# Stage 6 of a gated cross-attention network: PSUM dealt in single banks, and exponentials and maxima taken head by head

## The chip, the cores and the metric

The kernel runs on one core of one Trainium2 chip. The metric is the device time of one execution in microseconds, and smaller is better. The time of a kernel is the median of its runs; times are told in microseconds (us) throughout, durations of single instructions in us or ns.

## The reference

Four layers, each a cross-attention followed by a feed-forward, each added to x behind a tanh gate. The kernel works through them as stages 0 to 7; only stage 6, the attention of the last layer, is touched in what it computes. It is this function, on 4 batches of 512 tokens with 32 heads of 16 elements:

```python
def _L3_xattn_ref(x, ctx, pos_map, ctx_pos_map, Wq, Wkv, Wout, bout):   # x: layernormed (4, 512, 512), ctx: (4, 512, 256)
    q = (x @ Wq).reshape(b, n, 32, 16)
    k, v = jnp.split(ctx @ Wkv, 2, axis=-1)           # each (4, 512, 32 heads, 16)
    q = apply_axial_rope(q, pos_map)
    k = apply_axial_rope(k, ctx_pos_map)
    logits = jnp.einsum('bqhd,bkhd->bhqk', q, k) * 16 ** -0.5
    w = jax.nn.softmax(logits, axis=-1)
    attn = jnp.einsum('bhqk,bkhd->bqhd', w, v).reshape(b, n, 512)
    return attn @ Wout + bout
x = x + jnp.tanh(g_xattn[3]) * _L3_xattn_ref(...)
```

All of it is in float32.

## The kernel before, in words

A tile framework records the instructions in the order of the Python code, gives each a priority by that order, and then puts them into one fixed order for each engine; semaphores between the engines follow from the tiles that they share. So the order on an engine is fixed before the kernel starts, and an instruction that waits holds back all that stand behind it on that engine. `self.together` writes the matmuls of a group so that they start side by side (`tie` fixes their order among themselves), and `after` makes the first of the group wait for named instructions. `high_priority` moves an instruction ahead of others in its engine's order.

**Stage 6 (`s6`).** The keys with their rotation, transposed, and the values were made in earlier stages (`keys`, `keyT`) and lie in DRAM. Each head takes 32 rows of a 128-partition tile, so that four heads stand on four row groups of TensorE. Softmax needs the maximum over the keys, which the kernel gets from a first set of products, query by key (`ps`, in `maxima`): VectorE takes the negative maximum of each row (`tensor_reduce`, L1663), TensorE transposes it (`turn`, L1634), and VectorE adds it into a spare row of the query tile (L1639). The second set of products is key by query (`pl`, L1754 to L1763); with the spare row the maximum is subtracted in the product itself, and ScalarE takes the exponential (`prs`, L1769). `weigh` multiplies the exponentials by the values into `av`, `norm` transposes and divides, `project` and `projected` apply the output weights and add to x.

**The loop.** Over batch b (4), group g of four heads (8), block k of 128 keys (4) and pair i of heads (1, then 0): 256 *slots*. In each slot one group of four matmuls with 512 columns starts together: two `pl` products for this slot, and two `ps` products for a slot that lies LEAD = 12 slots ahead. They stand on the four different row groups. Then follow, on TensorE, what the slot has beside: after an i = 1 slot (called odd below) the four `av` products of the block before (`later`), after an i = 0 slot (even) what is in `behind` (`norm`, `project`, `projected`), a `turn`, or a piece of the next batch's queries from `todo`: `xT` (transposes of the layernormed x), `query` (a product of 4 matmuls, then six rotation instructions of VectorE, L1427 to L1429), `queryT` (eight transposes and two copies).

**PSUM.** Eight banks of 512 floats a partition. `ps4` holds one `pl` tile of two banks; `ps2` holds two tiles `sc` of two banks each, for the `ps` products and for the pieces `xT` and `queryT` (and for `query` of the first batch); `ps1` holds one bank `mm` (turns, norms, projections, later queries) and one bank `av`. One instruction of ScalarE reads both banks of a `pl` tile, one of VectorE both banks of a `ps` tile. A group's first matmul waits for the exponential of the slot before, as there is one `pl` tile, and, by `freed[-2:-1]`, for the maximum of two slots before.

```python
yield parts, freed[-2:-1], after              # L1668, freed: the reduces so far
self.together(parts + more, freed)            # L1765
nc.scalar.activation(prs[i], pl, AF.Exp)      # L1769, [128, 2, 512]
```

Of the kernel before, what the change touches and what calls it, by code (L numbers as in the profile page):

```python
# [9 lines left out]
F32 = mybir.dt.float32  # L10
# [5 lines left out]
AF = mybir.ActivationFunctionType  # L16
ALU = mybir.AluOpType
AX = mybir.AxisListType

P = 128  # L20
NB = 4
S = 512
# [26 lines left out]
class Net:  # L49
# [1390 lines left out]
                self.nc.gpsimd.memset(r[:, :, 16:17], fill)  # L1440
        return rooms

    def headsT(self, name, r, put):

        v = r.rearrange("p (g h) k -> p g (h k)", g=8)
        pt = self.sc(f"pt_{name}")
        for y in range(2):
            for i in range(4):
                self.nc.tensor.transpose(
                    pt[:, y, i * P : (i + 1) * P], v[:, 4 * y + i, :], self.ident  # L1450
                )
        put(pt)

    VW = 32 * 17 + 15

# [74 lines left out]
    def keyT(self, b, k, r):  # L1530
        kt = self.kp.tile([P, 8, P], F32, tag="kt", name=f"s6_kt_{b}_{k}", bufs=2)

        self.headsT(
            f"s6k_{b}_{k}", r,
            lambda pt: self.nc.scalar.mul(
                kt.rearrange("p (y g) n -> p y (g n)", y=2), pt, 16**-0.5
            ),
        )
        self.nc.sync.dma_start(self.k6[b][:, :, k * P : (k + 1) * P], kt)

    def s6(self):
        nc, a = self.nc, self.a
# [5 lines left out]
        ropes = self.padded("s6_q", 2, None)  # L1548
# [3 lines left out]
        ]  # L1552
        LEAD = 12
        made, stats = {}, {}

        top = [
            self.vp.tile([P, TB, 4, 32], F32, tag=f"top{i}", name=f"s6_top{i}", bufs=1)
# [5 lines left out]
        def pieces(b):  # L1563

            kT, qT = halves("kT", b), halves("qT", b)
            va = self.vp.tile([P, TB, VW], F32, tag="v", name=f"s6_v_{b}")
            made[b] = kT, qT, va
            for y in range(2):
                nc.sync.dma_start(kT[y], self.k6[b][:, 4 * y : 4 * y + 4, :])
            nc.sync.dma_start(va, self.v6[b].rearrange("(k p) n -> p k n", p=P))  # L1570
            xs = self.x[b * TB : (b + 1) * TB]
            room = {}
            cols = lambda k: slice(k * P, (k + 1) * P)

            def xT(y):
                if y == 0:
                    mv, rs = stats[b]
                    room["xl"] = []
                    for i, x in enumerate(xs):
                        xl = self.t(f"s6_xl_{b}_{i}")  # L1580
                        nc.vector.tensor_scalar(
                            xl, x, mv[:, i, 0:1], rs[:, i : i + 1], op0=ALU.subtract, op1=ALU.mult
                        )
                        room["xl"].append(xl)
                    room["xT"] = self.up.tile([P, DC, S], F32, tag="xT", name=f"s6_xT_{b}")
                pt = self.sc(f"s6_ptx_{b}_{y}")
                for i in range(2):
                    for t in range(TB):
                        nc.tensor.transpose(
                            pt[:, i, cols(t)], room["xl"][t][:, cols(2 * y + i)], self.ident  # L1590
                        )
                nc.scalar.copy(room["xT"][:, 2 * y : 2 * y + 2, :], pt)

            def query(t):
                if b:
                    pq = self.mm(f"s6_pq_{b}_{t}")
                else:

                    pq = self.sc(f"s6_pq_{b}_{t}")[:, 0, :]
                self.chain(pq, [(room["xT"][:, c, cols(t)], wq[:, c, :]) for c in range(DC)])  # L1600
                self.rope(f"q_{b}_{t}", pq, b * TB + t, ropes[t % 2])

            def results():

                self.combine("s5", self.wt5, range(b * TB, (b + 1) * TB))
                stats[b] = self.lnstats(
                    f"s6_{b}", self.x[b * TB : (b + 1) * TB], f"s6{b}", root=False
                )

            def queryT(t):  # L1610
                def put(pt):
                    for y in range(2):
                        nc.scalar.copy(
                            qT[y][:, :, cols(t)], pt[:, y, :].rearrange("p (g n) -> p g n", g=4)
                        )

                self.headsT(f"s6q_{b}_{t}", ropes[t % 2], put)

            out = [results, lambda: xT(0), lambda: xT(1)]
            for t in range(TB):  # L1620
                out.append(lambda t=t: query(t))
                if t:
                    out.append(lambda t=t: queryT(t - 1))
            return out + [lambda: None, lambda: queryT(TB - 1)]

        def maxima():

            freed = []

            def turn(b, g):  # L1630
                qT = made[b][1][g // 4]
                pt = self.mm(f"s6_ptm_{b}_{g}")
                for t in range(TB):
                    nc.tensor.transpose(  # L1634
                        pt[:, t * P : (t + 1) * P],
                        top[g % 2][:, t].rearrange("p j k -> p (j k)"),
                        self.ident,
                    )
                nc.vector.tensor_tensor(qT[:, g % 4, :], qT[:, g % 4, :], pt, op=ALU.add)  # L1639

            waiting = None
            for b in range(NB):
                kT, qT = made[b][0:2]
                for g in range(8):
                    for t in range(TB):
                        for y in range(2):
                            if waiting and t == 1:
                                turn(*waiting)
                                waiting = None
                            ps = self.sc(f"ps_s6_{b}_{g}_{t}_{y}")  # L1650
                            parts = []
                            for i in range(2):
                                rows = slice(32 * (2 * y + i), 32 * (2 * y + i + 1))
                                parts.append((
                                    ps[:, i, :],
                                    qT[g // 4][rows, g % 4, t * P : (t + 1) * P],
                                    kT[g // 4][rows, g % 4, :],
                                    dict(start=True, stop=True),
                                ))

                            def after(ps=ps, dst=top[g % 2][:, t, 2 * y : 2 * y + 2, 16:17]):
                                with self.tc.high_priority():
                                    i = nc.vector.tensor_reduce(  # L1663
                                        dst, ps, axis=AX.X, op=ALU.max, negate=True
                                    )
                                freed.append(i.ins)

                            yield parts, freed[-2:-1], after  # L1668
                    waiting = b, g
            turn(*waiting)  # L1670

        behind, later = Behind(), Behind()
        avs, o4s = {}, {}

        def flush(what):
            last, what.waiting = what.waiting, []
            for f, args in last:
                f(*args)

# [62 lines left out]
        for b in range(NB):  # L1742
# [4 lines left out]
            for g in range(8):  # L1747
                y, gi = g // 4, g % 4
                for k in range(TB):
                    prs = [None, None]  # L1750
                    for i in (1, 0):


                        pl = self.ps4.tile([P, 2, S], F32, tag="pl", name=f"pl_s6_{b}_{g}_{k}_{i}")  # L1754
                        parts = []
                        for j in (2 * i, 2 * i + 1):
                            rows = slice(32 * j, 32 * (j + 1))
                            parts.append((
                                pl[:, j % 2, :],
                                kT[y][rows, gi, k * P : (k + 1) * P],  # L1760
                                qT[y][rows, gi, :],
                                dict(start=True, stop=True),
                            ))  # L1763
                        more, freed, after = next(beside, None) or ([], [], None)
                        self.together(parts + more, freed)  # L1765
                        prs[i] = self.up.tile(
                            [P, 2, S], F32, tag="pr", name=f"pr_s6_{b}_{g}_{k}_{i}", bufs=4
                        )
                        nc.scalar.activation(prs[i], pl, AF.Exp)  # L1769
                        if after:  # L1770
                            after()
                        if i == 1:
                            flush(later)
                            later(weigh, b, g, k, prs, more=True)
                        else:
                            flush(behind)
                        slot += 1
                        while i == 0 and todo and (count - len(todo)) * room < slot * count:
                            todo.pop(0)()
# [72 lines left out]
def kernel(ctx: ExitStack, tc: tile.TileContext, a: dict, out: bass.AP):  # L1852
# [31 lines left out]
    net.y2 = 2  # L1884
    with net.pools(op=1, ep=4, bp=1, up=3, tp=8, sp=2, ps2=2, ps1=4):
        net.s5()
    with net.pools(wp=2, kq=4, vp=2, up=1, rp=1, tp=8, bp=1, sp=2, ps4=1, ps2=2, ps1=1):
        net.s6()
    net.y2 = 4
    with net.pools(op=1, wp=6, bp=1, up=6, tp=8, sp=2, ps2=2, ps1=4):  # L1890
# [84 lines left out]
```

## Time and profile before

| | |
|---|---|
| median of 3 runs | 3427.65 us (3422.73 to 3428.2) |
| the profiled execution, its own time | 3434.39 us |
| its span, first to last instruction | 3432.6 us |
| mean granted TensorE clock | 0.919 |
| TensorE busy (matmuls) | 2878.5 us, 84% |
| VectorE busy | 1960.6 us, 57% |
| ScalarE busy | 1180.2 us, 34% |
| stage 6: first of its transposes | 2282.20 us |
| stage 6: first and last exponential start | 2333.6 and 3016.2 us |

Times within the profile count from the first instruction. A row of the instruction groups has the line, the engine, the operation, what it writes and reads with the shape, how often, then its busy time, the mean duration of one, and the idle time of its engine just before them with what ended that idle time. A row of the timeline has the start, the duration from the first to the last of a merged run of instructions, the engine and the group. PE is TensorE (PEld its weight loads), DVE is VectorE, ACT is ScalarE, POOL is GpSimd, SP is SyncE. A float32 matmul shows as two records.

### The profile page before, as it was taken

How to read it: one execution, taken by the hardware profiler on the slowest of the kernel's cores; microseconds unless marked ns; L12 is line 12 of the kernel's file. 1: busy time of each engine (PE TensorE's matmuls, PEld its weight loads, DVE VectorE, ACT ScalarE, POOL GpSimd, SP SyncE). 2: the span in 40 equal slices, each digit the busy share in tenths (PEclk: the TensorE clock that was granted, in tenths of full speed). 3: DMA queues.
4: the chain of work that ended last, by engine and by line, in shares of the span. 5: the costliest groups of instructions: out<-in, count | busy, mean ns of one | idle time of the engine just before them, and what ended most of it. 6: DMA issues, size and time to landing. Idle time of an engine off the chain costs nothing.

```text
span 3432.6 us, 39483 instructions
## 1 busy us (share of the span) xinstructions
PE 2878.5 (84%) x14620; PEld 1422.3 (41%) x14624; DVE 1960.6 (57%) x2892; ACT 1180.2 (34%) x1663; POOL 626.3 (18%) x509
## 2 busy tenths in 40 slices
PE   4889898968899989998837699958888888889995
PEld 2333332223444444444415588832232322244673
DVE  5556555558898979975686211157555565434103
ACT  2243334355544444433222111113444344411231
POOL 0000000005564656650000122100000000000341
PEclk9799999978999999999967799988999999979997
DMA  3000000057676877851212799960000000022698
GB/s 124 7 1 7 1 1 9 1 181 222 196 233 177 229 204 232 243 168 56 75 60 93 236 325 320 316 216 11 13 27 13 26 1 1 1 74 77 232 384 318
DMA packets 266334, 438.52 MB, mean 128 GB/s; under 512 B 32368, under 2 KB 114544, under 8 KB 264608
## 3 DMA queue, kind: packets, MB, share of 16 engines
q1 hardware_dynamic: 247776, 382.52, 35.2%
q0 software_dynamic: 13760, 45.10, 3.6%
q10 hardware_dynamic: 4608, 8.39, 0.7%
q8 instruction: 116, 1.90, 0.2%
q14 instruction: 74, 0.61, 0.1%
HBM read 370.79 MB, written 65.13 MB: 127 GB/s over the span
## 4 chain that ended last, share of the span: by engine, by line
PE 35%; ACT 7%; DVE 6%; issue 3%; DMA 2%; POOL 2%; SPq 0%; POOLq 0%; ACTq 0%; DVEq 0%
PE s_po L238 8%; PE pl_s L262 8%; PE pg_s L238 6%; ACT pr_s L1769 6%; PE s_ph L238 2%; PE s_pq L238 2%; DVE x L729 1%; PE s_pr L238 1%; DMA s_y<-s_ys 1%; PE s_pkv L238 1%; PE pt_s L218 1%; POOL s_ys L1321 1%; PE s_av L262 1%; DVE st_s L175 1%; PE s_pb L238 1%
## 5 line engine op out<-in xcount | busy, mean ns | idle before, releaser
L262 PE MATMUL pl_s<-s_qT,s_kT 32*128 32x512 f32 (+1 forms) x1536 | 450.4, 663 | 128.3 <-ACT pr_s L1769 100.8
L1012 POOL TENSOR_TENSOR s_h<-s_h,s_C 128x512 f32<-128x512 f32 x256 | 445.7, 1741 | 300.8 <-DVE s_h L1011 261.6
L262 PE MATMUL ps_s<-s_kT,s_qT 32*128 32x512 f32 (+1 forms) x1536 | 453.9, 680 | 6.4 <-DVE s_nmx L599 4.1
L1663 DVE TENSOR_REDUCE s_top<-ps_s 128x2 f32<-128x1024 f32 x256 | 313.4, 1225 | 196.5 <-PE ps_s L262 196.3
L1769 ACT ACTIVATE pr_s<-pl_s 128x1024 f32<-128x1024 f32 x256 | 262.0, 1023 | 390.1 <-PE ps_s L262 359.4
L1011 DVE TENSOR_TENSOR_SCAN s_h<-s_da,s_db 128x512 f32<-128x512 f32 x256 | 311.9, 1218 | 62.8 <-PE s_y L262 36.9
L1010 ACT ACTIVATE s_da<-s_rdl,s_A 128x512 f32<-128x512 f32 x256 | 184.3, 722 | 333.0 <-DVE s_h L1011 331.0
L262 PEld LDWEIGHTS pl_s<-s_qT,s_kT 32*128 32x128 f32 (+1 forms) x1536 | 117.6, 187 | 408.9 <-ACT pr_s L1769 265.9
L238 PE MATMUL s_ph<-xT_s,s_wu 128*128 128x256 f32 x1024 | 248.4, 397 | 0.7 <-ACT xT_s L161 0.7
L771 PE MATMUL s_acc<-s_wd,s_hT 128*128 128x512 f32 x512 | 239.9, 612 | 6.7 <-ACT s_hT L802 6.7
L238 PEld LDWEIGHTS s_ph<-xT_s,s_wu 128*128 128x128 f32 x1024 | 198.4, 198 | 78.5 <-issue 48.3
L238 PEld LDWEIGHTS pg_s<-s_xbT,s_w 128*128 128x128 f32 (+1 forms) x1872 | 213.9, 183 | 19.8 <-issue 17.8
L599 DVE TENSOR_REDUCE s_nmx<-ps_s 128x2 f32<-128x992 f32 x128 | 151.3, 1184 | 119.3 <-PE ps_s L262 119.3
L238 PE MATMUL pg_s<-s_xbT,s_w 128*128 128x128 f32 (+1 forms) x1872 | 215.5, 275 | 1.4 <-ACT s_xbT L161 1.4
L262 PE MATMUL s_av<-pr_s,s_v 128*32 128x512 f32 (+1 forms) x1536 | 214.4, 632 | 1.2 <-ACT pr_s L1769 1.1
L1009 DVE TENSOR_TENSOR s_db<-s_B,s_rdu 128x512 f32<-128x512 f32 x256 | 204.3, 798 | 12.4 <-DMA s_B<-s_bc 4.6
L714 ACT ACTIVATE pr_s<-pl_s 128x1024 f32<-128x1024 f32 (+1 forms) x128 | 130.9, 1022 | 193.9 <-PE pl_s L262 163.5
L262 PE MATMUL s_y<-s_h,ident 64*64 64x512 f32 x1024 | 148.5, 643 | 51.4 <-issue 32.5
L1400 DVE TENSOR_TENSOR g_s<-g_s,pg_s 128x256 f32<-128x256 f32 x78 | 27.5, 352 | 263.8 <-ACT g_s L1399 263.8
L771 PEld LDWEIGHTS s_acc<-s_wd,s_hT 128*128 128x128 f32 x512 | 93.4, 192 | 151.9 <-issue 116.0
L1294 POOL DMA_INDIRECT s_xb<-s_xs,s_from x86 | 83.2, 967 | 371.6 <-PE ptr_s_xb L228 236.7
L1198 POOL IOTA s_js<- 128x39 f32 (+1 forms) x2 | 0.3, 174 | 778.9 <-PE s_po L238 778.9
(372 smaller groups left out, 4127.7 us busy)
## 6 DMA issues: line engine op xcount, KB each, us to landing
s_B<-s_bc SPq DMA_DIRECT2D x256, 256.0 KB, 4.9
s_C<-s_bc SPq DMA_DIRECT2D x256, 256.0 KB, 4.5
s_w<-in_s_wg SPq DMA_DIRECT2D x39, 704.0 KB, 4.8
s_w<-in_s_wu SPq DMA_DIRECT2D x39, 704.0 KB, 6.9
s_w_rt<-in_s_ru SPq DMA_DIRECT2D x47, 512.0 KB, 10.5
s_w_rt<-in_s_rd SPq DMA_DIRECT2D x47, 512.0 KB, 12.2
s_w<-in_s_wd SPq DMA_DIRECT2D x39, 512.0 KB, 8.4
s_y<-s_ys SPq DMA_DIRECT2D x32, 512.0 KB, 5.5
```

The costliest lines, as they stand in the source:

```text
L238: ins = self.nc.tensor.matmul(out, lhsT=l, rhs=r, start=(i == 0), stop=(i == len(pairs) - 1)).ins
L262: ins = self.nc.tensor.matmul(out, lhsT=l, rhs=r, **flags).ins
L599: i = nc.vector.tensor_reduce(nmx[:, at : at + 2], ps[:, :, 0:M], axis=AX.X, op=ALU.max, negate=True,)
L714: nc.scalar.activation(prs[i][0:n], pl[0:n], AF.Exp)
L771: ins = nc.tensor.matmul(accs[i][t], lhsT=hT[:, j, t * P : (t + 1) * P], rhs=wd[f // 4][:, f % 4, :], start=(f == 0), stop=(f == FC - 1),).ins
L1009: nc.vector.tensor_tensor(db, br, du, op=ALU.mult)
L1010: nc.scalar.activation(da, dl, AF.Exp, scale=am[:, e, n : n + 1])
L1011: nc.vector.tensor_tensor_scan(h, da, db, 0.0, op0=ALU.mult, op1=ALU.add)
L1012: nc.gpsimd.tensor_tensor(h, h, cr, op=ALU.mult)
L1294: self.nc.gpsimd.indirect_dma_start(out=t, out_offset=None, in_=self.sorted[name][1], in_offset=bass.IndirectOffsetOnAxis(ap=fr[:, j : j + ...
L1663: i = nc.vector.tensor_reduce(dst, ps, axis=AX.X, op=ALU.max, negate=True)
L1769: nc.scalar.activation(prs[i], pl, AF.Exp)
```

## The change

Stage 6's PSUM pools become one pool `ps3` with three buffers for each of two tags, every buffer a single bank: three banks `sc` for maxima and pieces, three banks `pl` for the weighed logits; `mm` and `av` stay. Every `pl` and `ps` product gets a bank of its own. The exponential and the maximum are taken by two instructions of 512 columns in place of one of 1024. A group's first matmul waits for `freed[-2:-1]` and `exps[-2:-1]`: as each slot now appends two entries, these are the first maximum and the first exponential of the slot just before. The pieces `xT` and `queryT` take two banks one after the other in place of one tile of two. `flush(behind, 2)` runs at most two of the waiting steps in a slot, and where nothing waited in `behind`, one more piece of `todo` is taken at once, so that the pieces come in earlier slots. `keyT` is written out in another way with the same instructions.

```diff
-    def headsT(self, name, r, put):
+    def headsT(self, name, r, y, pt):
         v = r.rearrange("p (g h) k -> p g (h k)", g=8)
-        pt = self.sc(f"pt_{name}")
-        for y in range(2):
-            for i in range(4):
-                self.nc.tensor.transpose(
-                    pt[:, y, i * P : (i + 1) * P], v[:, 4 * y + i, :], self.ident
-                )
-        put(pt)
+        for i in range(4):
+            self.nc.tensor.transpose(pt[:, i * P : (i + 1) * P], v[:, 4 * y + i, :], self.ident)
...
+        bank = lambda name: self.ps3.tile([P, S], F32, tag="sc", name=f"s6_{name}")
...
-                pt = self.sc(f"s6_ptx_{b}_{y}")
-                for i in range(2):
+                for c in (2 * y, 2 * y + 1):
+                    pt = bank(f"ptx_{b}_{c}")
                     for t in range(TB):
-                        nc.tensor.transpose(
-                            pt[:, i, cols(t)], room["xl"][t][:, cols(2 * y + i)], self.ident
-                        )
-                nc.scalar.copy(room["xT"][:, 2 * y : 2 * y + 2, :], pt)
+                        nc.tensor.transpose(pt[:, cols(t)], room["xl"][t][:, cols(c)], self.ident)
+                    nc.scalar.copy(room["xT"][:, c, :], pt)
...
             def queryT(t):
-                def put(pt):
-                    for y in range(2):
-                        nc.scalar.copy(
-                            qT[y][:, :, cols(t)], pt[:, y, :].rearrange("p (g n) -> p g n", g=4)
-                        )
-                self.headsT(f"s6q_{b}_{t}", ropes[t % 2], put)
+                for y in range(2):
+                    pt = bank(f"ptq_{b}_{t}_{y}")
+                    self.headsT(f"s6q_{b}_{t}", ropes[t % 2], y, pt)
+                    nc.scalar.copy(
+                        qT[y][:, :, cols(t)], pt.rearrange("p (g n) -> p g n", g=4)
+                    )
...
-                            ps = self.sc(f"ps_s6_{b}_{g}_{t}_{y}")
+                            ps = [bank(f"ps_{b}_{g}_{t}_{y}_{i}") for i in range(2)]
...
                             def after(ps=ps, dst=top[g % 2][:, t, 2 * y : 2 * y + 2, 16:17]):
-                                with self.tc.high_priority():
-                                    i = nc.vector.tensor_reduce(
-                                        dst, ps, axis=AX.X, op=ALU.max, negate=True
-                                    )
-                                freed.append(i.ins)
+                                for i in range(2):
+                                    with self.tc.high_priority():
+                                        ins = nc.vector.tensor_reduce(
+                                            dst[:, i], ps[i], axis=AX.X, op=ALU.max, negate=True
+                                        ).ins
+                                    freed.append(ins)
                             yield parts, freed[-2:-1], after
...
-        def flush(what):
-            last, what.waiting = what.waiting, []
+        def flush(what, n=None):
+            last, what.waiting = what.waiting[:n], what.waiting[n:] if n else []
...
-                        pl = self.ps4.tile([P, 2, S], F32, tag="pl", name=f"pl_s6_{b}_{g}_{k}_{i}")
+                        pl = [
+                            self.ps3.tile([P, S], F32, tag="pl", name=f"s6_pl_{b}_{g}_{k}_{i}_{j}")
+                            for j in range(2)
+                        ]
...
-                        self.together(parts + more, freed)
+                        self.together(parts + more, list(freed) + exps[-2:-1])
...
-                        nc.scalar.activation(prs[i], pl, AF.Exp)
+                        for j in range(2):
+                            exps.append(nc.scalar.activation(prs[i][:, j, :], pl[j], AF.Exp).ins)
...
-                            flush(behind)
+                            idle = not behind.waiting
+                            flush(behind, 2)
+                            if idle and todo:
+                                todo.pop(0)()
...
-    with net.pools(wp=2, kq=4, vp=2, up=1, rp=1, tp=8, bp=1, sp=2, ps4=1, ps2=2, ps1=1):
+    with net.pools(wp=2, kq=4, vp=2, up=1, rp=1, tp=8, bp=1, sp=2, ps3=3, ps1=1):
         net.s6()
```

More of the change, by code (lines that the diff above doesn't have):

```diff
@@ L1531, in keyT @@
         kt = self.kp.tile([P, 8, P], F32, tag="kt", name=f"s6_kt_{b}_{k}", bufs=2)
[L1533 to L1537, printed above, removed]
-        )
+        pt = self.sc(f"pt_s6k_{b}_{k}")
+        for y in range(2):
+            self.headsT(f"s6k_{b}_{k}", r, y, pt[:, y, :])
+        self.nc.scalar.mul(kt.rearrange("p (y g) n -> p y (g n)", y=2), pt, 16**-0.5)
         self.nc.sync.dma_start(self.k6[b][:, :, k * P : (k + 1) * P], kt)
@@ L1597, in query @@
                 else:
-                    pq = self.sc(f"s6_pq_{b}_{t}")[:, 0, :]
+                    pq = bank(f"pq_{b}_{t}")
                 self.chain(pq, [(room["xT"][:, c, cols(t)], wq[:, c, :]) for c in range(DC)])
@@ L1610, in queryT @@
             def queryT(t):
-                def put(pt):
-                    for y in range(2):
-                        nc.scalar.copy(
-                            qT[y][:, :, cols(t)], pt[:, y, :].rearrange("p (g n) -> p g n", g=4)
-                        )
-                self.headsT(f"s6q_{b}_{t}", ropes[t % 2], put)
+                for y in range(2):
+                    pt = bank(f"ptq_{b}_{t}_{y}")
[3 more added lines that the diff above has]
+                    )
             out = [results, lambda: xT(0), lambda: xT(1)]
@@ L1654, in maxima @@
                                 parts.append((
-                                    ps[:, i, :],
+                                    ps[i],
                                     qT[g // 4][rows, g % 4, t * P : (t + 1) * P],
@@ L1661, in after @@
                             def after(ps=ps, dst=top[g % 2][:, t, 2 * y : 2 * y + 2, 16:17]):
-                                with self.tc.high_priority():
-                                    i = nc.vector.tensor_reduce(
-                                        dst, ps, axis=AX.X, op=ALU.max, negate=True
-                                    )
-                                freed.append(i.ins)
+                                for i in range(2):
[4 more added lines that the diff above has]
+                                    freed.append(ins)
                             yield parts, freed[-2:-1], after
@@ L1672, in s6 @@
         behind, later = Behind(), Behind()
-        avs, o4s = {}, {}
-        def flush(what):
-            last, what.waiting = what.waiting, []
+        avs, o4s, exps = {}, {}, []
+        def flush(what, n=None):
+            last, what.waiting = what.waiting[:n], what.waiting[n:] if n else []
             for f, args in last:
@@ L1758, in s6 @@
                             parts.append((
-                                pl[:, j % 2, :],
+                                pl[j % 2],
                                 kT[y][rows, gi, k * P : (k + 1) * P],
```

## The prediction, made before the changed kernel ran

> **What bounds the kernel now.** I read the page's groups first, to see what stage 6 consists of and which engine waits for which; then the busy time by stretches, to see whether any engine is full; then the timeline of 12 us inside the loop, where the period can be read off. A row of the groups ends with the idle time before the instructions and who ended it.
>
> ```profile
> L262 PE MATMUL pl_s<-s_qT,s_kT 32*128 32x512 f32 (+1 forms) x1536 | 450.4, 663 | 128.3 <-ACT pr_s L1769 100.8
> L1663 DVE TENSOR_REDUCE s_top<-ps_s 128x2 f32<-128x1024 f32 x256 | 313.4, 1225 | 196.5 <-PE ps_s L262 196.3
> L1769 ACT ACTIVATE pr_s<-pl_s 128x1024 f32<-128x1024 f32 x256 | 262.0, 1023 | 390.1 <-PE ps_s L262 359.4
> ...
> L1613 ACT COPY s_qT<-pt_s6q 128x512 f32<-128x512 f32 x32 | 17.2, 588 | 19.5 <-PE pt_s6q L1449 19.5
> L163 DVE COPY xT_s<-pt_s 128x512 f32<-128x512 f32 x32 | 21.3, 685 | 32.5 <-PE pt_s L218 32.5
> ```
>
> TensorE waits for the exponential and the exponential waits for TensorE: a ring. The last two rows are the nearest to the new halves: 512 columns read from PSUM cost 0.588 us on ACT and 0.685 on DVE.
>
> ```profile
> 2400.00:2500.00 100.00, 81.91 (x572) 25.63 (x568) 59.86 (x68) 47.62 (x53) 0.00 (x0) 1.00 0.07 21
> 2800.00:2900.00 100.00, 85.64 (x560) 27.08 (x556) 57.95 (x61) 44.08 (x49) 0.00 (x0) 1.00 0.00 1
> ```
>
> Columns: width, then busy PE, PEld, DVE, ACT, POOL, then granted clock. No engine is full and the clock is 1.00.
>
> ```profile
> 2422.24 0.70 PE L262 MATMUL pl_s<-s_qT,s_kT 32*128 32x512 f32 x2 [0.17 <-ACT pr_s L1769]
> 2423.41 1.02 ACT L1769 ACTIVATE pr_s<-pl_s 128x1024 f32<-128x1024 f32 x1 [0.70 <-PE ps_s L262]
> 2423.47 1.23 DVE L1663 TENSOR_REDUCE s_top<-ps_s 128x2 f32<-128x1024 f32 x1 [1.09 <-PE ps_s L262]
> 2424.49 0.70 PE L262 MATMUL pl_s<-s_qT,s_kT 32*128 32x512 f32 x2 [0.52 <-ACT pr_s L1769]
> ...
> 2425.56 3.70 PE L238 MATMUL s_pq<-s_wq,s_xT 128*128 128x512 f32 x8
> ...
> 2429.19 1.06 PE L262 MATMUL s_av<-pr_s,s_v 128*32 128x512 f32 x8
> 2429.30 0.42 DVE L1427 TENSOR_TENSOR rt_q<-s_pq,s_sin 128x256 f32<-128x256 f32 x1 [2.35 <-PE s_pq L238]
> ...
> 2430.19 0.70 PE L262 MATMUL pl_s<-s_qT,s_kT 32*128 32x512 f32 x2
> ...
> 2431.09 0.42 DVE L1429 TENSOR_TENSOR s_q_r<-s_q_r,rt_q 128x256 f32<-128x256 f32 x1
> 2431.36 1.02 ACT L1769 ACTIVATE pr_s<-pl_s 128x1024 f32<-128x1024 f32 x1 [4.61 <-PE ps_s L262]
> 2431.43 1.22 DVE L1663 TENSOR_REDUCE s_top<-ps_s 128x2 f32<-128x1024 f32 x1
> 2432.44 0.70 PE L262 MATMUL pl_s<-s_qT,s_kT 32*128 32x512 f32 x2 [1.11 <-ACT pr_s L1769]
> 2433.51 1.07 PE L262 MATMUL s_av<-pr_s,s_v 128*32 128x512 f32 x8
> ...
> 2434.75 0.70 PE L262 MATMUL pl_s<-s_qT,s_kT 32*128 32x512 f32 x2 [0.17 <-ACT pr_s L1769]
> ```
>
> A group starts at 2422.24, its exponential 1.17 later (1.23 in other slots) and takes 1.02, the next group starts 0.06 after its end: 2.25; the slot from 2432.44 takes 2.31. Reading the whole loop this way, slots without large work alternate 2.31 (odd) and 2.25 (even). TensorE itself needs less: a group holds it 1.07 (2424.49 to 2425.56), a query 3.63 (to 2429.19), `av` 1.00 (to 2430.19). An odd slot on TensorE alone is 1.07 + 1.00 = 2.07. Slots with a query or a projection (4.70, or 5.70 with `av`) are TensorE's already.
>
> **The change part by part.**
>
> *The ring.* With three banks a slot needs one bank that is free and one that the first half-read of the slot before gives back. So the period becomes 1.23 + one half-read + 0.05. For ACT 0.588: 1.87. For DVE 0.69 (its tensor-tensor rows from PSUM cost 691 ns for 512 columns and 424 for 256, 1.04 ns a column, and 1.225 less 512 of these is 0.69; the copy is 0.685): 1.97, later than ACT. An odd slot is then TensorE's, 2.07; an even slot without large work is DVE's, 1.97. A pair goes from 4.56 to 4.04. The reduce of 512 columns isn't in the trace; its bounds are 0.57 (taking off at the rate between the 992- and 1024-column reduces, 1184 and 1225 ns, 1.28 ns a column) and 0.79 (the same 0.1 on the other side); I take 0.69, on which two rows agree. At 0.57 ACT's 1.87 is the limit.
>
> *The second halves.* In the trace two copies in a row take 1.07 together, so the pair of exponentials costs 1.07 against 1.02, and rotation instructions of DVE follow each other 0.08 before the last one's end, so the pair of maxima takes 1.30 against 1.225: 256 x 0.05 = 13 us on ACT and 256 x 0.075 = 19 on DVE. Nobody waits for the second half before the slot after next: it ends 2.53 after the group's start, the next maximum is due at 1.97 + 1.23 = 3.20. Cover: the next group's 1.23. Were it gone, each slot would pay 0.61.
> Here a rule speaks against the change. The Trainium skill, "TensorEngine Tiling (Array Packing)", section PSUM Bottleneck, advises to "Vectorize PSUM access across multiple tiles in same bank", and "Advanced Engine Details and Errata", section The Read-Write Bubble, advises large tiles because each instruction exposes the memory latency anew, and says that one instruction may read several banks: what the kernel before does. By the rule the split loses the larger of 13 and 19 us, which makes 3447, if these engines set the time. The rows say that ACT is 44 to 48% and DVE 58 to 60% busy here, and that what counts is the time to the first bank's release. I follow the rows.
>
> *What the lost slot of slack costs.* Before, a group waited for the maximum of two slots ago; now for that of the last. What stands on DVE ahead of a maximum now holds TensorE, and with it all that is queued behind the group: `av`, turns, transposes. In the order of the changed program the six rotations of a query stand ahead of the next slot's maxima. They start 0.11 after the query's end and let the next DVE instruction start 2.24 after it (2431.43 against 2429.19). The query now ends an even slot, so the next group starts at its end; its first maximum ends at 2.24 + 0.69 = 2.93, and the slot takes 2.98 in place of 2.07: 12 queries inside the loop. Norms (0.25 + 0.42) and turns (0.68) stand behind both maxima on DVE and end by 3.2, just when the next is due: nothing.
>
> *The pieces in single banks.* `queryT` takes two of three `sc` banks. The second must wait for the slot's first maximum (1.97), its transposes end at 2.40, and the next group's second `ps` product waits for the copy of the first, which stands on ACT behind both exponentials (1.23 + 0.49 + 0.49 = 2.21, plus 0.59, plus 0.05 = 2.85). I take 2.80 for such a slot, 3.05 with a turn behind it (0.64), against 2.25 and 2.53 before; bounds: 1.97 if the scheduler's order dodges the wait, 3.3 if it waits for the second copy. `xT` the same.
>
> *The new distribution.* In the order of the changed program all queries stand alone in even slots (4.70) where 9 of 12 stood with `av` (5.70). That only moves `av`; the sum below counts it.
>
> *Elsewhere.* keyT issues the same instructions. No DMA is added or moved past another; the loads of the next batch keep their place, and the DMA engines are nearly idle here (share 0.00 to 0.07).
>
> **The sum.** From the start at 2344.70 of one odd slot to that at 2978.60 lie 239 slots, 633.9 us. By the order of the changed program they are:
>
> - 98 odd with `av` alone at 2.07: 202.9
> - 12 odd after a query at 2.98: 35.8
> - 82 even (35 empty, 30 norms, 17 turns) and 3 with transposes of the output at 1.97: 167.4
> - 12 queries at 4.70: 56.4
> - 8 `queryT` at 2.80, 4 with a turn at 3.05, one `xT` at 3.1: 37.7
> - 7 projections at 4.70, 3 with `av` at 5.70, 5 slots of transposes and `av` (four at 2.65, one at 3.37, as before): 64.0
> - 4 mixed slots at batch changes, before 5.76 and 6.21, estimated 6.2 and 6.5: 25.4
>
> Together 589.6, a gain of 44.3. At the start of the loop, up to 2345, DVE sets the pace (residuals and maxima in a row), and the split costs 16 slots x 0.075 = 1, an earlier `xT` 0.5. At the end, ten slots without `ps` took 3.2 and 3.87 at a lower clock; five even ones save 1.02 - 0.59 = 0.43: 2. Gain 45. Against the profiled execution's 3434.4 that is 3389; it is 6.7 above the median of the runs, 3427.65, from which 3383 follows.
>
> **The rivals.**
>
> *DVE becomes the pacemaker (slower).* Its other work in a batch is about 38 us (rotations 4 x 2.2, turns 8 x 0.68, norms 8 x 0.67, projections 4 x 1.44, layernorm 4 x 0.54, the rest spread): 0.59 a slot. A maximum may be 2.28 - 1.97 = 0.31 late on average before the gain of a slot is gone. If all that work came ahead of maxima, a slot would take 1.97 + 0.59 = 2.56, 0.28 more than now in some 210 slots: +59, 3486. For it: DVE goes from 58 to some 82% of the shorter time, and the slack is one slot less. Against: the order puts nearly all but the rotations and a few projections behind the maxima.
>
> *Half the gain.* The piece slots wait for the second copy (13 x 0.5), and the even slots take 2.15 (83 x 0.18), because semaphores and two waits of a group add up: gain 23, 3405. For it: the 1.23 was never measured with two readers in a row on each engine.
>
> *More.* The half maximum takes 0.57, even slots 1.87 (85 x 0.1), the pieces dodge their wait (12 x 0.6): gain 60, 3368.
>
> *It does not do what it says:* the banks rotate so that a group needs the bank of the second read. Then a slot is 1.23 + 1.30 + 0.05 = 2.58, slower by about 60 as well. Against: each slot takes two of three banks and the pieces take two, so the first bank taken is always the one that is free.
>
> The granted clock could fall in a denser stage, but the stretch before stage 6 has TensorE 100% busy at 1.00, so no time is set on it.
>
> **How the numbers follow.** Forecast (gain 35 to 55) 0.58, half the gain 0.18, more 0.13, pacemaker 0.05, wrong rotation 0.03, no measurable change 0.03. A measurement of this kernel can tell about 0.2%, 7 us, from no change. Faster 0.88, same 0.04 (with the lowest end of half the gain, 0.01), slower 0.08. The range goes from the larger gain, with 4 us beyond it, to a gain of 17: 3364 to 3411.
>
> **What would show it.** In the changed profile: pairs of slots at 4.04; ACT rows of 128x512 at 0.59 and maxima at 0.69; the group's idle time ended by DVE's maximum in even slots and none in odd ones; slots after queries near 3.0; `queryT` slots near 2.8; stage 6 ending near 2975. Wrong if maxima start well after 1.23, if even slots stay at 2.2, or if the clock in 2400 to 2900 leaves 1.00.

## Result and the profile after

| | before | after |
|---|---|---|
| time, median of 4 runs each | 3426.32 us | 3398.16 us (3392.73 to 3401.39) |
| ratio | | 0.9917, 95% interval 0.99 to 0.9935 |
| span of the profiled execution | 3432.6 us | 3399.4 us |
| mean granted clock | 0.919 | 0.92 |

Faster by 28 us by the medians and by 33.2 us by the two profiled spans, where 44 to 45 were forecast. The time lies inside the range, and the mechanism is the one forecast, but the sum is made up differently.

The groups of the kernel after, from the page: busy time, mean ns of one instruction, then the idle time before it and who ended it.

```profile
L1656 DVE TENSOR_REDUCE s_top<-s_ps 128x1 f32<-128x512 f32 x512 | 330.1, 686 | 162.6 <-PE s_ps L262 158.4
L1766 ACT ACTIVATE pr_s<-s_pl 128x512 f32<-128x512 f32 x512 | 277.9, 595 | 344.2 <-PE s_ps L262 327.1
L262 PE MATMUL s_pl<-s_qT,s_kT 32*128 32x512 f32 x1024 | 291.4, 642 | 63.4 <-DVE s_top L1656 59.0
```

The halves cost what was assumed (686 ns for 0.69 us, 595 for 0.588). In the last row ACT no longer ends the group's waits: 59.0 of 63.4 us of them are now ended by the maximum. Before, in a row that holds products of other stages too, the exponential of stage 6 ended 100.8 of 128.3 us. The ring through the exponential is cut.

The busy time of the same two stretches as before (width, PE, PEld, DVE, ACT, POOL, granted clock, DMA share, GB/s):

```profile
2400.00:2500.00 100.00, 86.70 (x627) 27.15 (x620) 67.08 (x113) 54.81 (x101) 0.00 (x0) 1.00 0.03 11
2800.00:2900.00 100.00, 89.74 (x592) 28.64 (x588) 64.78 (x106) 49.81 (x93) 0.00 (x0) 1.00 0.00 1
```

TensorE rises from 82 to 87 and from 86 to 90. DVE stays below 70%, so it did not become the pacemaker.

The timeline of two slots of the loop after, an empty even one and an odd one with `av`:

```profile
2440.97 0.70 PE L262 MATMUL s_pl<-s_qT,s_kT 32*128 32x512 f32 x2
...
2442.12 1.08 ACT L1766 ACTIVATE pr_s<-s_pl 128x512 f32<-128x512 f32 x2 [1.01 <-PE s_ps L262]
2442.21 1.29 DVE L1656 TENSOR_REDUCE s_top<-s_ps 128x1 f32<-128x512 f32 x2 [0.81 <-PE s_ps L262]
2443.05 0.70 PE L262 MATMUL s_pl<-s_qT,s_kT 32*128 32x512 f32 x2 [0.94 <-DVE s_top L1656]
...
2444.12 1.06 PE L262 MATMUL s_av<-pr_s,s_v 128*32 128x512 f32 x8
...
2445.11 0.70 PE L262 MATMUL s_pl<-s_qT,s_kT 32*128 32x512 f32 x2
```

A DVE or ACT row with x2 is a pair of half instructions: 1.29 for the maxima, 1.08 for the exponentials. The even slot lasts 2443.05 - 2440.97 = 2.08: 1.24 to the maximum's start, 0.69 for its first half, and 0.15 to the next group, where the forecast had 0.05. The odd slot, 2.06 here and 2.08 on average, is TensorE's own. A pair is 4.14 to 4.16 instead of 4.56; 4.04 was forecast.

Where the 33.2 us of the spans come from, stage by stage (times read from the two timelines):

| stretch | before | after | gain | forecast |
|---|---|---|---|---|
| up to the first transposes of stage 6 | 2282.20 | 2283.28 | -1.1 | 0 |
| from there to slot 5 of the loop (the lead) | 62.5 | 74.55 | -12.0 | -1.5 |
| slots 5 to 243 (the loop) | 633.9 | 602.7 | 31.2 | 44.3 |
| slot 244 to the last group (the tail) | 35.5 | 23.4 | 12.1 | 2 |
| last group to the end (mostly stage 7) | 418.4 | 415.4 | 3.0 | 0 |

So the experiments had four questions: which half of the change makes the loop's gain, what the lead lost, what the tail gained, and why even slots take 2.08.

### The profile page after: what moved, and what is told of

Its sections match the earlier page's. It is cut to its first block, busy times and chain, and to the rows that moved or that the text cites. A ratio compares the mean times of both kernels' runs of the same rounds, so it can differ in the third digit from the quotient of the medians.

```text
span 3399.4 us, 39917 instructions
## 1 busy us (share of the span) xinstructions
PE 2880.1 (85%) x14620; PEld 1432.3 (42%) x14624; DVE 1975.8 (58%) x3148; ACT 1197.1 (35%) x1927; POOL 627.9 (18%) x509
## 4 chain that ended last, share of the span: by engine, by line
PE 38%; DVE 9%; issue 3%; DMA 2%; POOL 2%; ACT 1%; SPq 0%; POOLq 0%; DVEq 0%; ACTq 0%
PE s_po L238 8%; PE s_pl L262 7%; PE pg_s L238 6%; PE s_av L262 4%; DVE s_top L1656 2%; PE s_ph L238 2%; PE s_pq L238 2%; PE s_ps L262 1%; PE s_pkv L238 1%; PE s_pr L238 1%; DVE x L729 1%; DMA s_y<-s_ys 1%; PE pt_s L218 1%; POOL s_ys L1321 1%; PE s_pb L238 1%
## 5 line engine op out<-in xcount | busy, mean ns | idle before, releaser
L1656 DVE TENSOR_REDUCE s_top<-s_ps 128x1 f32<-128x512 f32 x512 | 330.1, 686 | 162.6 <-PE s_ps L262 158.4
L1766 ACT ACTIVATE pr_s<-s_pl 128x512 f32<-128x512 f32 x512 | 277.9, 595 | 344.2 <-PE s_ps L262 327.1
L262 PE MATMUL s_pl<-s_qT,s_kT 32*128 32x512 f32 x1024 | 291.4, 642 | 63.4 <-DVE s_top L1656 59.0
L262 PE MATMUL s_ps<-s_kT,s_qT 32*128 32x512 f32 x1024 | 306.6, 668 | 6.1 <-DVE s_top L1656 5.8
L1009 DVE TENSOR_TENSOR s_db<-s_B,s_rdu 128x512 f32<-128x512 f32 x256 | 202.7, 792 | 10.5 <-DMA s_B<-s_bc 2.7
L262 PEld LDWEIGHTS s_pl<-s_qT,s_kT 32*128 32x128 f32 x1024 | 80.0, 184 | 232.9 <-ACT pr_s L1766 197.7
L262 PE MATMUL pl_s<-s_qT,s_kT 32*128 32x512 f32 (+1 forms) x512 | 151.1, 667 | 26.1 <-ACT pr_s L714 23.0
L262 PE MATMUL ps_s<-s_kT,s_qT 32*128 32x496 f32 x512 | 156.1, 713 | 4.5 <-DVE s_nmx L599 4.1
```

The source lines that it names most:

```text
L262: ins = self.nc.tensor.matmul(out, lhsT=l, rhs=r, **flags).ins
L1009: nc.vector.tensor_tensor(db, br, du, op=ALU.mult)
L1656: ins = nc.vector.tensor_reduce(dst[:, i], ps[i], axis=AX.X, op=ALU.max, negate=True).ins
L1766: exps.append(nc.scalar.activation(prs[i][:, j, :], pl[j], AF.Exp).ins)
```

## The experiments

Each time is the median, each ratio is to the kernel before timed on the same chip; runs e1 to e4 shared one chip and its runs of the kernel before, e5 to e7 another, e8 a third.

**e1: the lead on two kinds of banks.** In the lead the `pl` banks are idle. Its maxima take `sc` and `pl` banks in turn, and each group waits for the slot before the last, as it did before the change.

```
-                             ps = [bank(f"ps_{b}_{g}_{t}_{y}_{i}") for i in range(2)]
+                             tag = "pl" if count < LEAD and count % 2 else "sc"
+                             ps = [bank(f"ps_{b}_{g}_{t}_{y}_{i}", tag) for i in range(2)]
...
-                             yield parts, freed[-2:-1], after
+                             yield parts, freed[-4:-3] if count < LEAD else freed[-2:-1], after
+                             count += 1
```

> The changed kernel, but the twelve groups of maxima ahead of the loop take their two banks in turn from the three sc banks and from the three pl banks, which nothing else uses then, and wait for the maximum of two slots before. Theory 1 (the ring of one slot costs 12 us ahead of the loop: a group of 2.08 at half clock, a half maximum of 0.69 and 0.08 in a row, 2.85 a slot): the first exponentials' group starts 10 to 12 us earlier, 3387 if the changed kernel is at 3398. Rival (VectorE's own work, about 24 us of residuals and maxima, or the half clock sets the pace there whatever the banks): less than 3 us, 3396.

Measured 3387.67 us (3384.98 to 3393.58), ratio 0.9893 (0.9877 to 0.991). The first `pl` group comes 46.8 us after the first transposes; it was 58.8 in the kernel after and 49.3 in the kernel before. Up to slot 5 it is 63.4, against 74.55 in the kernel after and 62.5 in the kernel before, so 11.1 of the 12.0 us are back. Loop 604.0, tail 23.4. The interval of the ratio just overlaps that of the kernel after (0.99 to 0.9935); the stages decide it. The lead's loss was the single-slot distance. The timeline of the kernel after shows it:

```profile
2315.57 1.29 DVE L1656 TENSOR_REDUCE s_top<-s_ps 128x1 f32<-128x512 f32 x2 [0.83 <-PE s_ps L262]
2316.32 2.08 PE L262 MATMUL s_ps<-s_kT,s_qT 32*128 32x512 f32 x4 [0.37 <-DVE s_top L1656]
2318.42 1.29 DVE L1656 TENSOR_REDUCE s_top<-s_ps 128x1 f32<-128x512 f32 x2 [0.82 <-PE s_ps L262]
2319.17 2.08 PE L262 MATMUL s_ps<-s_kT,s_qT 32*128 32x512 f32 x4 [0.78 <-DVE s_top L1656]
```

There is no `av` to fill the wait, and the group, here two products (four records), takes 2.08 at a clock near 0.50, where a group of the loop takes 1.07 at 1.00. From group to group 2319.17 - 2316.32 = 2.85: matmul and half maximum stand in a row, and nothing overlaps. The same stretch by busy time (columns as above), first of the kernel before:

```profile
2309.00:2331.00 22.00, 20.16 (x58) 6.29 (x56) 20.82 (x42) 2.36 (x3) 0.00 (x0) 0.64 0.24 72
```

Of the kernel after:

```profile
2308.00:2342.00 34.00, 27.17 (x55) 7.08 (x53) 24.45 (x57) 2.12 (x3) 0.00 (x0) 0.51 0.24 77
```

Of e1:

```profile
2307.00:2327.00 20.00, 17.80 (x48) 5.74 (x45) 19.28 (x46) 0.64 (x1) 0.00 (x0) 0.50 0.17 57
```

DVE is busy 20.82 of 22 us before, 24.45 of 34 after, and 19.28 of 20 again in e1. The lead's bound is DVE, as the prediction said, but only while TensorE runs a slot ahead of it. The granted clock of 0.50 costs nothing in e1, since DVE covers it; with the shorter distance it stands in the chain.

**e2: one wait less.** The group's first matmul no longer asks for the exponential's end by itself.

```
-                         self.together(parts + more, list(freed) + exps[-2:-1])
+                         self.together(parts + more, freed)
```

> The changed kernel without the added wait for the first exponential at a group's first matmul (the second matmul still waits for it, as it reuses that bank). In the changed kernel a group starts 0.15 after the first half maximum in the loop and 0.06 after it ahead of the loop, where no exponential is waited for. Theory 1 (two waits at one matmul are worked off one after the other and cost 0.09): even slots go from 2.08 to about 1.99, 85 of them, a gain of 8 us, 3390. Rival (the 0.15 is the maximum's own signal, or the wait that the second matmul keeps costs the same): even slots stay at 2.08, 3398.

Measured 3392.99 us (3390.01 to 3399.22), ratio 0.9911 (0.9896 to 0.9926); by the time alone that can't be told from the kernel after. The slots tell more: loop 599.7 for 602.7. Slots with norms fell to 2.00 from 2.08, slots with `av` after a query to 2.98 from 3.07, but empty slots and turns stayed at 2.08. The timeline of e2 has both kinds, a norm slot that ends at 2451.72 (it began at 2449.73) and an empty one from 2453.78:

```profile
2450.97 1.29 DVE L1656 TENSOR_REDUCE s_top<-s_ps 128x1 f32<-128x512 f32 x2 [0.81 <-PE s_ps L262]
2451.72 0.70 PE L262 MATMUL s_pl<-s_qT,s_kT 32*128 32x512 f32 x2 [0.26 <-DVE s_top L1656]
...
2453.78 0.70 PE L262 MATMUL s_pl<-s_qT,s_kT 32*128 32x512 f32 x2
...
2455.03 1.29 DVE L1656 TENSOR_REDUCE s_top<-s_ps 128x1 f32<-128x512 f32 x2 [0.78 <-PE s_ps L262]
2455.86 0.70 PE L262 MATMUL s_pl<-s_qT,s_kT 32*128 32x512 f32 x2 [0.94 <-DVE s_top L1656]
```

From the pair of maxima to the next group: 0.75 behind the norm, 0.83 behind the empty slot. The first `pl` product needs a bank that an exponential has read. Behind a norm, TensorE has already waited for a later instruction of ACT (the copy that feeds the norm's transposes), so the product waits for DVE alone; behind an empty slot or a turn it has not, and the same matmul still waits for ACT and DVE.

The records of the traces show the second wait itself, which the timeline leaves out: an instruction of its own (EVENT_SEMAPHORE, 0.05 us) in TensorE's queue, which waits for DVE ahead of the group's first weight load, while the weight load waits for ACT. In slots 5 to 243 TensorE stood idle ahead of 92 groups of the kernel after; all have this instruction, and all start 0.15 behind the last release. In e2, 57 have it and start 0.15 behind; 35 don't and start 0.05 to 0.06 behind. In the kernel before, 187 of 188 don't and start 0.05 to 0.06 behind. So the expectation held for one kind of slot only, and the edit was too weak for the others. e8 comes back to it.

**e3 and e4: the distribution.** e3 is the kernel after with the distribution of before; e4 is the kernel before with the new distribution alone. The cut is from e3; e4 has it the other way round.

```
-                            idle = not behind.waiting
-                            flush(behind, 2)
-                            if idle and todo:
-                                todo.pop(0)()
+                            flush(behind)
```

> The changed kernel with the distribution of the steps as in the kernel before: everything waiting in behind runs at once, and no piece is taken early. Theory 1 (a query that stands alone in an even slot saves nothing here, as the rotations then hold the next slot's maxima: 4.70 + 3.07 against 5.70 + 2.08): by the slots' sizes 604 against 603 us in the loop, 3399, no difference. Rival (the distribution is part of the gain): 8 to 12 us slower than the changed kernel, 3408.

> The kernel before with the new distribution alone; banks, exponentials and maxima as before. Theory 1 (with two slots of slack the rotations hold nobody up, and a query in an even slot hides the 2.25 wait of that slot instead of adding to an odd one): by the slots' sizes 622 against 634 us in the loop, a gain of 12, 3414. Rival (the order of the pieces doesn't matter, the banks make the whole gain): 3426.

e3 measured 3400.84 us (3395.1 to 3403.7), ratio 0.9926 (0.9913 to 0.9939): the kernel after within its error. e4 measured 3423.48 us (3412 to 3434), ratio 0.9995 (0.9982 to 1.0008): no change. e4's profiled loop takes 628.2, from 633.9 before, instead of the 622 expected: a turn behind a query waits for the one `mm` bank until the rotations have read it, and such slots take 3.59. So the times show no effect of the distribution, and the interval of e4 leaves room for at most 6 us. The profiled loops are a little shorter with it in both kernels: by 5.7 us in e4, and by 5.3 us in the kernel after, against 608.0 in e3. Of the 5.3, 2.7 lie in slots 5 and 6 of e3, where the granted clock was 0.50 for 6.8 us. These are single traces; the distribution may hold a small part of the loop's 31.2 us, and the banks and the split reads hold the rest.

**e5: the maxima alone.** The kernel after with one double `pl` tile, one exponential of 1024 columns and the distribution of before.

```
-                        pl = [
-                            self.ps3.tile([P, S], F32, tag="pl", name=f"s6_pl_{b}_{g}_{k}_{i}_{j}")
-                            for j in range(2)
-                        ]
+                        pl = self.ps4.tile([P, 2, S], F32, tag="pl", name=f"pl_s6_{b}_{g}_{k}_{i}")
...
-                        for j in range(2):
-                            exps.append(nc.scalar.activation(prs[i][:, j, :], pl[j], AF.Exp).ins)
+                        nc.scalar.activation(prs[i], pl, AF.Exp)
```

> The kernel after, but the pl group keeps its one double tile of two banks and its one exponential of 1024 columns; only the sc tiles are dealt in single banks (three), with the maxima and the pieces split. Theory 1 (the loop's period was set by the ring of the exponential, and the split maxima are only what has to follow once that ring is cut): slots stay at 2.31 and 2.25, a pair near 4.56, the loop keeps its 634 us or loses some to the slots after queries; the lead still pays its 12 us, since it waits for the half maximum of the slot just before; in all about 3437 us, slower than the kernel before by about 10. Rival (the maxima's earlier release makes the gain): pairs near 4.15 and a time near 3400.

Measured 3455.57 us (3449.33 to 3458.08), ratio 1.0072 (1.006 to 1.0085): slower than the kernel before by 25 us. The timeline of e5:

```profile
2446.74 1.02 ACT L1762 ACTIVATE pr_s<-pl_s 128x1024 f32<-128x1024 f32 x1 [4.61 <-PE s_ps L262]
2446.80 1.28 DVE L1656 TENSOR_REDUCE s_top<-s_ps 128x1 f32<-128x512 f32 x2
2447.82 0.70 PE L262 MATMUL pl_s<-s_qT,s_kT 32*128 32x512 f32 x2 [1.11 <-ACT pr_s L1762]
```

The exponential ends at 2447.76, the group starts 0.06 later. Slots are 2.31 and 2.25 to the hundredth, as before: the ring is whole, and split maxima bring nothing by themselves. They cost: the lead 74.0 (11.5 more than before), the 12 slots with `queryT` and a turn 2.99 where they had 2.53 (5.5 us), the mixed slots at batch changes 6.96 where two had 5.76 (2.4); these three are 19.4 of the 20.8 us between the two profiled spans. The expectation had the sign and the loop's pair right and left out the pieces' wait, 7.9 us, which is part of why it said 10. In the terms of the rule that the prediction weighed ("TensorEngine Tiling (Array Packing)", section PSUM Bottleneck, and "Advanced Engine Details and Errata", section The Read-Write Bubble, in the Trainium skill): reading one instruction's worth in two costs 0.06 (ACT) and 0.065 (DVE) a pair here. The second page's own sizes for large tiles are 512 or 1024 elements, so a half of 512 is within its advice. The price of the split is not what made e5 slower; the shorter distance in the lead and the pieces' waits for banks are. No run splits the exponentials alone.

**e6: the tail with four row groups.** The kernel before; where no products for maxima are left, two unread products fill the other two row groups.

```
+                        if not more:
+                            idle = self.sc(f"fill_{b}_{g}_{k}_{i}")
+                            for j in (2 - 2 * i, 3 - 2 * i):
+                                rows = slice(32 * j, 32 * (j + 1))
+                                more.append((
+                                    idle[:, j % 2, :],
+                                    qT[y][rows, gi, k * P : (k + 1) * P],
+                                    kT[y][rows, gi, :],
+                                    dict(start=True, stop=True),
+                                ))
                         self.together(parts + more, freed)
```

> The kernel before; in the last slots of stage 6, in which no products for maxima are left, the group of two products on two row groups gets two more beside them on the other two row groups, written to a free sc tile and read by nobody (work added, outputs unchanged). Theory 1 (the tail of the kernel before is slow because TensorE's clock falls when only two of four row groups work, and the 12 us of the tail are a matter of the clock, not of split exponentials): granted clock in the last 30 us of stage 6 stays near 1.00 in place of 0.50 to 0.55, slots there take 2.3 in place of 3.2 to 3.9, the tail goes from 35 to about 25 us, time near 3416. Rival (the clock follows the idle gaps of TensorE in each slot, which the ring of the exponential leaves either way): clock and tail as before, 3426. With the rival true the tail's gain belongs to the split exponentials after all.

Measured 3419.55 us (3412.74 to 3428.83), ratio 0.9971 (0.9963 to 0.9979): 10 us faster than the kernel before by adding work. The tail by busy time (columns as above), first of the kernel before:

```profile
2990.00:3000.00 10.00, 9.92 (x34) 2.43 (x34) 0.68 (x2) 3.65 (x4) 0.00 (x0) 0.55 0.01 2
3000.00:3014.00 14.00, 11.75 (x36) 2.38 (x32) 0.00 (x0) 4.09 (x4) 0.00 (x0) 0.50 0.00 0
```

Of e6:

```profile
2980.00:2990.00 10.00, 7.60 (x57) 1.97 (x57) 0.85 (x2) 4.09 (x4) 0.00 (x0) 1.00 0.00 0
2990.00:3003.00 13.00, 9.73 (x76) 2.67 (x76) 0.68 (x2) 6.67 (x7) 0.00 (x0) 1.00 0.01 1
```

Of the kernel after:

```profile
2970.00:2984.00 14.00, 12.20 (x66) 3.16 (x66) 0.68 (x2) 8.74 (x17) 0.00 (x0) 1.00 0.00 1
```

The clock is 0.50 to 0.55 before and 1.00 in e6, and the slots of e6 keep 2.31 and 2.25 to the end, with pauses of TensorE of about 1.1 us in the even slots without a norm in both kernels. So two row groups with these pauses brought the clock down, and four with the same pauses don't. The tail falls from 35.5 to 27.4: 8.1 of the tail's 12.1 us are the clock. The other 4.0 (27.4 to 23.4) are the split exponentials, which shorten the slots to 2.06 and 1.80. The clock reaches beyond the tail: in the 46 us behind the last group it is 0.89 in e6 and 0.77 in the kernel before, and from the last group to the end e6 takes 412.5, the kernel before 418.4. In the tail of the kernel after, two row groups with these shorter pauses also keep 1.00; where between the two the line lies, these runs don't say.

**e7: e1 and e2 together.** The edits of e1 and e2 in one kernel.

> The kernel after with both changes at once: the lead's maxima take sc and pl banks in turn and wait for the slot before the last, and the group's first matmul no longer asks for the exponential's end by itself. If the two are independent, 10.5 and 5 us add up: 3383 us, and the loop near 600 with the first pl group 47 us after the first transposes. Rival (the shorter lead only moves work into the loop, or the wait taken away is worth nothing): 3388.

Measured 3384.56 us (3383.1 to 3386.33), ratio 0.9866 (0.9852 to 0.988). The lead is 46.7 us to the first `pl` group. Norm slots are at 2.00, `av` after a query at 2.98. The profiled loop is 604.1, not 600: one slot at a change of batches took 9.79 instead of 6.96. The granted clock was 0.50 there for 6.8 us, from 2506.23; no other stretch of this loop lies below 1.00. TensorE had not stood idle for more than 0.39 us in that slot before the clock fell; why it fell stays open.

**e8: the maxima's products first.** The kernel of e7 with the order of a group's four products turned around, so that the first matmul waits for DVE alone and the wait for ACT stands on a later one.

```
-                         self.together(parts + more, freed)
+                         self.together(more + parts, freed)
```

> The kernel of the run with both changes (lead on two kinds of banks, no explicit wait for the exponential), with the four products of a group in another order: the two for maxima first, the two weighed logits behind them. The first matmul of a group then waits for DVE alone, and the wait for the exponential stands on the group's last matmul, where it has long ended. Theory (two waits at one matmul cost about 0.08 more than one): the 35 empty slots and 17 turn slots fall from 2.08 to 2.00 as the norm slots did before, or lower, since the maxima start some 0.06 sooner: to about 1.94; 52 times 0.08 to 0.14 is 4 to 7 us, the loop falls to about 596 and the time to about 3379. Rival (the empty and turn slots are longer for another reason, such as the moment at which the maximum itself starts): they stay at 2.08, time 3385. Exponentials start 0.06 later, which nobody waits for by either theory.

Measured 3378.71 us (3369.72 to 3382.43), ratio 0.9844 (0.9822 to 0.9866). Two consecutive groups of e8's timeline, around a slot with a norm:

```profile
2439.76 0.70 PE L262 MATMUL s_ps<-s_kT,s_qT 32*128 32x512 f32 x2
...
2440.92 1.29 DVE L1658 TENSOR_REDUCE s_top<-s_ps 128x1 f32<-128x512 f32 x2 [0.78 <-PE s_pl L262]
2441.01 1.08 ACT L1769 ACTIVATE pr_s<-s_pl 128x512 f32<-128x512 f32 x2 [0.50 <-PE s_pl L262]
2441.67 0.70 PE L262 MATMUL s_ps<-s_kT,s_qT 32*128 32x512 f32 x2 [0.18 <-DVE s_top L1658]
```

The maximum starts 1.16 after the group instead of 1.24, and the next group comes 0.75 after the maximum: 1.91. Empty slots and turns are now 1.90 as well, and so are 26 of the 30 norms (1.90 to 1.91): the three kinds are alike once no group begins with two waits. Of 87 groups that TensorE stood idle for, one still has the extra instruction; the others start 0.05 to 0.06 behind the release. From 2.08, 0.08 is the earlier maximum and 0.09 the wait (0.15 to 0.06).

So the even slots fell lower than the theory's 1.94, and the time is the 3379 expected, but not by the sum that was expected. The loop takes 599.8, not 596, and 2.8 of the 4.3 us gained on e7 are its slow slot at 2506. What the even slots won was lost behind the queries. In the order of e8 a maximum stands on DVE ahead of the last three rotations. A slot with `av` alone after a query gains from it (2.07 for 2.98 in e7), but a turn, which waits for the rotations, comes later:

```profile
2398.93 1.09 PE L1627 MATMUL s_ptm<-ident,s_top 128*128 128x128 f32 x4 [2.12 <-DVE s_q_r L1428]
2399.94 1.94 PE L262 MATMUL s_av<-pr_s,s_v 128*32 128x512 f32 x8
```

Right behind this wait of 2.12 the granted clock is 0.50 for 3.4 us: the turn takes 1.09 for 0.66 and `av` 1.94 for 1.06. Five such slots last 5.48 to 6.15 each, where e7 has 3.56 to 3.63. e8 is the best version that was run, 53 us below the kernel before by the ratio (1.56% of 3427.65), where the change alone brings 28; its ratio and that of e7 overlap at the ends of their intervals.

## Why the prediction was right, and where its sum was off

Right were the bound (the ring through the exponential), its cure and the sign. e5 shows it from the other side: with the ring left whole, the rest of the change costs 25 us (without the distribution, which by e3 and e4 is worth a few us at most). The price of the half instructions was right, and so was their cover: wherever TensorE stood idle ahead of a group of the loop, it was a first half that ended last.

Term by term, against a forecast of 44.8 (44.3 - 1.5 + 2) and 33.2 from the stages:

- **Even slots without large work, 1.97 each.** Measured 2.08: 85 x 0.11 = 9.3 us less gain. The failing step is the "+ 0.05" of the period. It was read from groups of the kernel before, which wait for one thing that ends late; `self.together(..., list(freed) + exps[-2:-1])` puts two waits ahead of the first matmul, and the second is an instruction more. e2 and e8 show 0.06 with one wait and 0.15 with two. The rival "half the gain" had named it ("semaphores and two waits of a group add up") and had put it at 2.15.
- **Slots after a query, 2.98.** Seven with `av` alone 3.07, five with a turn 3.59: 3.7 us less. Of this 7 x 0.09 is the same second wait; the other five hold the turn behind the rotations, for the `mm` bank. The prediction had named the rotations, but let only the maxima wait for them.
- **Piece slots.** `queryT` 2.58 for 2.80, with a turn 2.99 for 3.05, `xT` 2.78 for 3.1: 2.3 us more gain. The wait for the piece's copy came as forecast, but it holds only the last product of the next group, 0.18 us in the odd slot behind: eight of these last 2.24 to 2.25.
- **Odd slots** 2.08 for 2.07 (1.4 us, in these eight alone), projections and mixed slots: together 2.6 less. With the three items above, 44.3 becomes 31.0, and 31.2 was measured.
- **The lead, -1.5.** Measured -12.0: the largest single miss. The step said that DVE sets the pace there, and priced only the second halves. It applied the lost slot of slack to the loop and not to the lead, where each group has nothing beside it. e1 gives the time back.
- **The tail, +2.** Measured +12.1: e6 splits it into 8.1 for the granted clock and 4.0 for the exponentials. The step had seen "a lower clock" in the tail and left it as it was; it set no time on the clock, and that was wrong here to the kernel's favour. It read ten slots as slow; only the last six take 3.2 or 3.87, as the clock falls during the fourth.
- **From the last group to the end**, +3.0, was not in the sum. Its first 46 us run at a granted clock of 0.88 in place of 0.77 (the windows from 2984 and from 3014). e6, which changes the tail alone, has 0.89 there and gains 5.9, so this too seems to go with the clock of the tail.

The misses of the lead (10.5 too good) and the tail (10.1 too bad) cancel almost exactly, and that is luck: the two have different causes. What remains of the gap is the loop: 13.1 us, of which 8.3 are the second wait (92 slots x 0.09). Of the rivals, the pacemaker and the wrong rotation did not occur, and "more" failed because the half maximum takes 686 ns and ends behind ACT's.

## What to carry to other kernels

Split a read of PSUM where its first release closes the ring. With the ring whole the split of e5 won nothing in the loop, and dealing the banks singly spent slack (a slot's distance) that other stretches of the program, such as a pipeline's filling, had lived on. Before pricing a change by its steady state, walk through the filling and the emptying too: here they moved by -12 and +12 us. Where two waits meet at the head of a chain, order the work so that its first instruction waits for the later of the two alone, and look at what else the new order moves: in e8 it delayed the turns.

## What the runs showed of the hardware

- A matmul that waits for ACT and DVE, DVE ending last, starts 0.15 us after DVE's end, with one wait 0.06 us (even slots of the kernel after against norm slots of e2 and even slots of e8). The second wait is an instruction of its own in TensorE's queue.
- TensorE's granted clock went to 0.50 while it worked in every slot, with pauses of about 1.1 us in every second slot and two of four row groups filled (tail of the kernel before); filling the other two row groups with unread products, at the same pauses, kept it at 1.00 and made the kernel 10 us faster (e6). Shorter pauses alone did so too (tail of the kernel after).
- The clock of 0.50 cost nothing in the lead of e1, where DVE is full, and 12 us in the lead of the kernel after together with the missing distance: a low clock counts only where TensorE is in the chain.
- In e8 TensorE stood idle for 2.12 us ahead of a turn, and its granted clock was 0.50 for the next 3.4 us.
